# Two layers on one core: layer 0 split into a front and a back, with the dense steps of two batches dealt out over the stages

## The chip, the core and the metric

The kernel runs on one core of a Trainium2 chip. The core has TensorE (PE, matrix products into PSUM; its weight loads are listed apart as PEld), VectorE (DVE), ScalarE (ACT), GpSimd (POOL), SyncE (SP, which issues most DMAs here) and 16 DMA engines. Each engine works through its own list of instructions in order, and semaphores hold an instruction back until its inputs are there. PSUM has eight banks of 512 float32 columns. All data are float32, and each float32 product appears in the trace as two passes of PE.

The metric is the time of one execution on the device in microseconds; the median of three runs stands for a kernel.

## What is computed

The input x has 4 batches of 512 tokens with 256 features. Two layers follow one another:

```python
xn = _layernorm(x)
x = x + _L0_attn_ref(xn, ...) + _L0_ffn_ref(xn, ...)     # layer 0
xn = _layernorm(x)
x = x + _L1_attn_ref(xn, ...) + _L1_ffn_ref(xn, ...)     # layer 1
```

Layer 0's attention is linear: q, k and v are projections of xn; phi is elu + 1; the running sum of phi(k)·v over the tokens is multiplied by phi(q), scaled by 0.25 and projected by Wo. Layer 0's second part scores each token against 512 genes (logits = xn·Wc), keeps the 32 largest, takes their softmax, mixes the 32-wide gene vectors with it, and forms tanh(mix·Wd)·xn·(mix·Wu)·scale.

Layer 1's first part projects to q, k, v, forms running sums of exp(k)·v and exp(k), divides them, multiplies by sigmoid(q), and sends the result through a gated unit of width 1024. Its second part is a shared gated unit of width 352 and a choice of 2 among 16 experts of width 176 for each token.

## The kernel before, in words

Tokens stand on the 128 partitions, so that a batch has four tiles of 128 tokens. `xs` holds x and every result added to it; x of batch 0 is loaded first (`load_x(0)`, L110), then the weights, and x of batches 1 to 3 behind all weights (L148-149). SP's queue ends with a write of zeros to the 6016 KB of expert rows in DRAM (L173). Weights that layer 0 alone needs are in pool `wp`, on the right side of SBUF, and layer 0's working tiles in the pools `io0` (two buffers of each name) and `one0` (one).

The work is written as Python generators that yield after each step:

- `layer0(b, i0, nt)` (L224) does layer 0 for nt tiles of batch b from tile i0. It takes statistics (L194: bn_stats, bn_aggr, a square root on ACT) and normalises (L211), transposes by PE (`turn`, L217, its matmuls on L221) and copies to `xnT`. Then, tile by tile: `logits` (L286: two products of 512 columns, L289, copied by ACT to `lg`, of which there are two buffers); `top` (L296: four rounds of MAX8 and MATCH_REPLACE8 on DVE, L301 and L302, the exponential on ACT into a tile `e`, L307, and the masked sum, L309); a share of the attention parts `attend_kv` and `attend_q` (L265, L278: projections on L244, `phi` on ACT and DVE, a scan over the tokens on L271); and `express` (L313: four transposes of `e`, products with the genes, L321, and with Wd and Wu, L324, tanh, L326, a product on DVE, L329, and four elementwise operations on POOL, L331-334). `out` (L336) adds the projected context to `xs` for each tile at the end. Where a batch is cut in two, the running sum is handed on in `carry` (L275).
- `mix(b, i0, nt)` (L361) does layer 1 up to yT, the gate's input, and the choice of experts: statistics, normalise, transposes, q, k, v and the expert scores (L384), squares, exponentials (L410-411), four scans over transposed data (L421), reciprocals (L430) and the pick of two experts (L450-456).
- `dense(b, half, busy)` (L566) does the gated units of half a batch: 11 chunks (3 shared ones that read only the transposed xn of mix, then 8 that read yT). A chunk is an `up` (four products, L578, tanh on ACT, L582, a product on DVE, L584, and with `busy` a copy on ACT, L586, and a product on POOL, L587, else a product on DVE, L589) and, two chunks later, a `down` (L595). Its PSUM tiles `gu` are in `ps_d` (three banks) and `acc` in `ps_a` (one). Layer 0 and mix share the other four banks (`bank`, L188).
- `route`, `scatter`, `experts` and `combine` do the experts. Scatter's 32 DMAs and the loading of the expert weights are `paced`: each waits for the `down` that was written last before it.

`together` (L43) merges streams: it always takes the next step of the stream that has done the smallest share of the number given with it. The stages (L633-669) are:

```python
together(a(0, 0, 2))                              # a is layer0, m is mix, d is dense
together(m(0, 0, 2), a(0, 2, 2))
together(m(0, 2, 2), a(1, 0, 4), d(0, 0))
together(m(1, 0, 4), a(2, 0, 4), d(0, 1))
together(m(2, 0, 4), a(3, 0, 4), d(1, 0))
together(m(3, 0, 4), d(1, 1), (load_experts(), 17))
```

Between the second and third ACT halves two weight matrices (L636-639), and after the fifth the right side of SBUF is given to the expert weights (`first.close()`, L643, and a memset on POOL, L650). Then come routing with dense (2, ·), scatter with the rest of it, the experts, and combine with dense (3, ·).

What is written first has precedence, but the order on an engine is not exactly the order of the text: the framework that builds the program plans each engine's list ahead of time, and takes later work early where its inputs and its buffers should be there. The trace shows it: statistics of batch 1 (third stage) stand on DVE at 38.7 us, before batch 0 has been through mix.

Of the kernel before, what the change touches and what calls it, by code (L numbers as in the profile page):

```python
# [11 lines left out]
F32 = mybir.dt.float32  # L12
# [4 lines left out]
P = 128  # L17
# [36 lines left out]
def tile_two_layers(  # L54
# [47 lines left out]
    def load_x(b):  # L102
        nc.sync.dma_start(xs[:, b], x[b].rearrange("(t p) d -> p t d", p=P))
# [28 lines left out]
    nc.sync.dma_start(bob, bo0.partition_broadcast(P))  # L132
    wot = wp.tile([P, NH, D], F32, name="wot")
    nc.sync.dma_start(wot, wo0.rearrange("(h p) e -> p h e", p=P))

    w1 = const.tile([P, NH, 3 * D + NE], F32, name="w1")
    nc.sync.dma_start(w1[:, :, 0 : 3 * D], wqkv1.rearrange("(h p) e -> p h e", p=P))
# [48 lines left out]
    one = first.enter_context(tc.tile_pool(name="one0", bufs=1, side="right"))  # L186

    def bank():  # L188
        return ps_m.tile([P, L], F32, name="pm")
# [21 lines left out]
    def normalise(to, b, i0, nt, mv, rs):  # L211
        for i in range(nt):
            V.tensor_scalar(  # L213
                to[:, i], xs[:, b, i0 + i], mv[:, i, 0:1], rs[:, 0, i : i + 1], ALU.subtract, ALU.mult
            )

    def turn(src, nt, at):  # L217

        pt = bank()
        for i in range(nt):  # L220
            T.transpose(pt[:, i * P : (i + 1) * P], src[:, i, at : at + P], ident)  # L221
        return pt[:, 0 : nt * P]

    def layer0(b, i0, nt):  # L224

        W = nt * P
        mv, rs = statistics(io, b, i0, nt)
        xn = io.tile([P, NT, D], F32, name="xn")
        normalise(xn, b, i0, nt, mv, rs)

        sl = io.tile([P, 2, NT], F32, name="sl")
        V.tensor_scalar(sl[:, 0, 0:nt], rs[:, 1, 0:nt], rtemp, None, ALU.mult)
        V.tensor_scalar(sl[:, 1, 0:nt], rs[:, 1, 0:nt], scl, None, ALU.mult)
        yield
        xnT = io.tile([P, NH, L], F32, name="xnT")
        for h in range(NH):
            S.copy(xnT[:, h, 0:W], turn(xn, nt, h * P))
        yield


        def project(c):
            pm = bank()[:, 0:W]
            for h in range(NH):
                T.matmul(  # L244
                    pm,
                    wqkv[:, h, c * P : (c + 1) * P],
                    xnT[:, h, 0:W],
                    start=(h == 0),
                    stop=(h == NH - 1),
                )  # L250
            return pm

        def phi(c):

            pm = project(c)
            e = io.tile([P, L], F32, name="phi", bufs=3)[:, 0:W]
# [5 lines left out]
        ctxT = one.tile([P, NH, L], F32, name="ctxT")  # L262
        cums = {}

        def attend_kv(h):  # L265
            fk = phi(2 + h)
            pv = project(4 + h)
            kv = one.tile([P, L], F32, name="kv")[:, 0:W]
            V.scalar_tensor_tensor(kv, pv, bqkv[:, 4 + h : 5 + h], fk, ALU.add, ALU.mult)
            cum = io.tile([P, L], F32, name="cum")[:, 0:W]  # L270
            V.tensor_tensor_scan(  # L271
                cum, ones[:, 0:W], kv, carry[:, h : h + 1] if i0 else 0.0, ALU.mult, ALU.add
            )
            if i0 + nt < NT:
                V.tensor_copy(carry[:, h : h + 1], cum[:, W - 1 : W])  # L275
            cums[h] = cum

        def attend_q(h):  # L278
            fq = phi(h)
            V.scalar_tensor_tensor(ctxT[:, h, 0:W], fq, QSCALE, cums[h], ALU.mult, ALU.mult)  # L280


        rden = io.tile([P, NT], F32, name="rden")
        exT = one.tile([P, L], F32, name="exT")

        def logits(i):  # L286
            pl = bank()
            for h in range(NH):
                T.matmul(  # L289
                    pl, xnT[:, h, i * P : (i + 1) * P], wct[:, h], start=(h == 0), stop=(h == NH - 1)  # L290
                )
            lg = io.tile([P, NG], F32, name="lg")
            S.copy(lg, pl)  # L293
            return lg

        def top(i, lg):  # L296
# [12 lines left out]
            V.scalar_tensor_tensor(e, rep, TAKEN, e, ALU.is_equal, ALU.mult, accum_out=den)  # L309
            V.reciprocal(rden[:, i : i + 1], den)  # L310
            return e

        def express(i, e):  # L313
# [8 lines left out]
            S.copy(exT[:, i * P : (i + 1) * P], px[:, 0:P])  # L322
            du = bank()
            T.matmul(du, exT[:, i * P : (i + 1) * P], wdut, start=True, stop=True)  # L324
# [8 lines left out]
            G.tensor_tensor(xs[:, b, i0 + i], xs[:, b, i0 + i], bob, ALU.add)  # L333
            G.tensor_tensor(xs[:, b, i0 + i], xs[:, b, i0 + i], dn, ALU.add)

        def out(i):  # L336
            ao = bank()[:, 0:D]
            for h in range(NH):
                T.matmul(
                    ao, ctxT[:, h, i * P : (i + 1) * P], wot[:, h], start=(h == 0), stop=(h == NH - 1)  # L340
                )
            V.tensor_tensor(xs[:, b, i0 + i], ao, xs[:, b, i0 + i], ALU.add)


        parts = [lambda h=h, f=f: f(h) for h in range(NH) for f in (attend_kv, attend_q)]
        lg = logits(0)
        for i in range(nt):
            nxt = logits(i + 1) if i + 1 < nt else None
            e = top(i, lg)
            yield  # L350
            for part in parts[i * len(parts) // nt : (i + 1) * len(parts) // nt]:
                part()
            yield
            express(i, e)
            lg = nxt
            yield
        for i in range(nt):
            out(i)
            yield

# [260 lines left out]

    H = NC + 1

    def a(b, i0, nt):
        return layer0(b, i0, nt), 2 + 4 * nt

    def m(b, i0, nt):
        return mix(b, i0, nt), 6 + nt

    def d(b, half, busy=True):  # L630
        return dense(b, half, busy), H
# [12 lines left out]

    we = ctx.enter_context(tc.tile_pool(name="we", bufs=1, side="right"))
# [226 lines left out]
```

## Time and profile before

The three timed runs gave 593.17, 593.67 and 596.4 us. The profiled execution is another one:

| | us |
|---|---|
| median of the timed runs | 593.67 |
| the profiled execution's own time | 600.39 |
| its span, from first to last instruction | 598.7 |
| PE busy in the span | 541.2 |
| DVE busy in the span | 375.1 |
| first instruction of PE (L221) | 9.2 |
| first `top` of tile 0 / of tile 2 of batch 0 | 14.5 / 53.4 |
| last operation of mix of batch 3 (L432) ends | 344.1 |
| last dense (2, ·) product, end of the scatter's stage | 400 |
| experts begin / combine begins | 410 / 528 |

Busy time is time in which an engine has an instruction under way; matmuls overlap, and their ends are modelled, so that a busy PE is not always at its pace. Idle time has a releaser: what ended the wait. The chain of waits goes back from the last instruction, at each step to what released it; in it PE has 60% of the span, DVE 23%, ACT 6%, DMA 4% and POOL 2%. The largest groups are the dense products (L578, 125.6 us busy), those of the experts (L735, 64.8 us) and the downs (L595, 66.5 us). On DVE, MAX8 and MATCH_REPLACE8 of `top` take 685 and 675 ns each, 64 times each.

### The profile page before, as it was taken

What the parts mean: (1) busy time and instruction counts of PE and PEld (TensorE: products, weight loads), DVE (VectorE), ACT (ScalarE), POOL (GpSimd) and SP (SyncE); (2) the same over time, 40 slices, a digit from 0 to 9 for tenths busy, and PEclk for the clock granted to TensorE, in tenths of its full rate; (3) what the DMA queues carried; (4) which work ended last, traced back from release to release, by engine and by line L of the source; (5) the groups of instructions that cost most, each with busy time, mean ns of one, the idle gap of its engine ahead of it and who ended that gap; (6) DMA issues with size and microseconds to landing.
All of it is one profiled execution on the core that took longest, in us unless ns stands there. A gap on an engine that the chain in (4) does not pass through costs nothing.

```text
span 598.7 us, 7339 instructions
## 1 busy us (share of the span) xinstructions
PE 541.2 (90%) x2384; PEld 394.7 (66%) x2384; DVE 375.1 (63%) x992; ACT 233.1 (39%) x528; POOL 171.8 (29%) x214
## 2 busy tenths in 40 slices
PE   3557899989999999999999999898999999997796
PEld 1334665658566775667767788675777777785585
DVE  4979999997896888968923982231222222234552
ACT  2454755743556525565247111113333333321010
POOL 1234223252221532214532126650000000036640
PEclk9688999999999999999999999997999999999899
DMA  5993000000000000000086502223333332124431
GB/s 160 384 380 112 1 1 1 2 0 1 1 1 0 1 1 1 1 1 1 1 246 184 150 10 96 89 88 109 115 106 108 108 106 80 53 80 123 125 105 36
DMA packets 38373, 47.39 MB, mean 79 GB/s; under 512 B 3936, under 2 KB 34880, under 8 KB 38080
## 3 DMA queue, kind: packets, MB, share of 16 engines
q1 hardware_dynamic: 35264, 38.53, 19.9%
q0 software_dynamic: 3072, 8.39, 4.5%
q8 instruction: 20, 0.33, 0.2%
q14 instruction: 17, 0.14, 0.1%
HBM read 28.30 MB, written 18.61 MB: 78 GB/s over the span
## 4 chain that ended last, share of the span: by engine, by line
PE 60%; DVE 23%; ACT 6%; issue 4%; DMA 4%; POOL 2%; SPq 0%; DVEq 0%; ACTq 0%; POOLq 0%
PE gu L578 16%; PE pu L735 10%; PE acc L595 9%; PE py L756 7%; PE pm L384 5%; PE pt L698 4%; PE pm L244 3%; DVE sums L430 3%; DVE rep L302 3%; DVE top L301 3%; PE pm L289 2%; DVE sums L421 2%; DMA xg<-yrows,slot 2%; PE pm L324 2%; DVE xn L213 1%
## 5 line engine op out<-in xcount | busy, mean ns | idle before, releaser
L578 PE MATMUL gu<-yT,wugt 128*128 128x256 f32 x512 | 125.6, 381 | 0.0
L578 PEld LDWEIGHTS gu<-yT,wugt 128*128 128x128 f32 x512 | 95.2, 190 | 19.5 <-issue 7.4
L582 ACT ACTIVATE th<-gu 128x256 f32<-128x256 f32 (+1 forms) x88 | 32.9, 382 | 131.1 <-PE gu L578 85.5
L595 PE MATMUL acc<-wot,hid 128*128 128x256 f32 x256 | 66.5, 386 | 10.4 <-issue 4.5
L802 POOL DMA_INDIRECT xg<-yrows,slot x32 | 30.3, 948 | 144.9 <-DVE hid L589 130.8
L584 DVE SCALAR_TENSOR_TENSOR th<-th,gu 128x256 f32<-128x256 f32 (+1 forms) x88 | 35.9, 411 | 56.1 <-ACT th L582 50.8
L735 PE MATMUL pu<-wex,xgT 128*128 x188 | 64.8, 467 | 0.0
L595 PEld LDWEIGHTS acc<-wot,hid 128*128 128x128 f32 x256 | 47.7, 190 | 22.5 <-issue 6.7
L587 POOL TENSOR_TENSOR hid<-hid,th 128x256 f32<-128x256 f32 (+1 forms) x44 | 33.7, 770 | 95.6 <-ACT hid L586 95.6
L244 PE MATMUL pm<-xnT,wqkv 128*128 128x512 f32 (+1 forms) x120 | 46.7, 529 | 4.7 <-ACT lg L293 1.7
L744 DVE TENSOR_TENSOR hb<-pu,hb 128x176 f32<-128x176 f32 x47 | 16.1, 341 | 50.7 <-ACT hb L743 50.7
L578 PE MATMUL gu<-xn1T,sgu 128*128 128x256 f32 (+1 forms) x192 | 47.8, 393 | 0.0
L384 PE MATMUL pm<-w,xn1T 128*128 128x512 f32 (+1 forms) x128 | 45.8, 501 | 0.0
L756 PE MATMUL py<-wex,hgT 128*128 x188 | 44.5, 379 | 0.0
L756 PEld LDWEIGHTS py<-wex,hgT 128*128 128x128 f32 x188 | 35.6, 190 | 8.6 <-issue 0.2
L578 PEld LDWEIGHTS gu<-xn1T,sgu 128*128 128x128 f32 (+1 forms) x192 | 35.6, 189 | 7.3 <-issue 0.9
L735 PEld LDWEIGHTS pu<-wex,xgT 128*128 128x128 f32 x188 | 32.7, 194 | 10.2 <-issue 0.5
L384 PEld LDWEIGHTS pm<-w,xn1T 128*128 128x128 f32 x128 | 24.6, 193 | 22.2 <-issue 19.0
L244 PEld LDWEIGHTS pm<-xnT,wqkv 128*128 128x128 f32 x120 | 23.8, 201 | 22.6 <-issue 13.7
L748 DVE COPY hgT<-pt 128x512 f32<-128x512 f32 (+1 forms) x24 | 16.3, 680 | 34.9 <-PE pt L698 34.9
L544 POOL DMA_INDIRECT xrows<-xn,slot x32 | 30.9, 967 | 25.1 <-DVE cpair L538 9.7
L301 DVE MAX8 top<-rep 128x8 f32<-128x512 f32 x48 | 32.8, 685 | 0.4
(162 smaller groups left out, 881.2 us busy)
## 6 DMA issues: line engine op xcount, KB each, us to landing
xrows<-zero SPq DMA_DIRECT2D x1, 6016.0 KB, 22.6
xg<-xrows SPq DMA_DIRECT2D x23, 256.0 KB, 2.7
yrows<-yg SPq DMA_DIRECT2D x23, 256.0 KB, 2.1
wex<-in_w_gate_up_dram SPq DMA_DIRECT2D x8, 704.0 KB, 4.5
xs<-in_x_dram SPq DMA_DIRECT2D x4, 512.0 KB, 7.9
wugt<-in_wug_dram SPq DMA_DIRECT2D x1, 2048.0 KB, 12.2
wex<-in_w_down_dram SPq DMA_DIRECT2D x4, 512.0 KB, 4.9
out_dram<-xs SPq DMA_DIRECT2D x4, 512.0 KB, 2.9
```

Of the source, the lines that this page charges most:

```text
L244: T.matmul(pm, wqkv[:, h, c * P : (c + 1) * P], xnT[:, h, 0:W], start=(h == 0), stop=(h == NH - 1),)
L301: V.max(tp[:, 8 * r : 8 * r + 8], src)
L384: T.matmul(o[:, 0:n], xnT[:, h, i * P : (i + 1) * P], w1[:, h, at : at + n], start=(h == 0), stop=(h == NH - 1),)
L544: sc = G.indirect_dma_start(out=xrows, out_offset=bass.IndirectOffsetOnAxis(ap=slot[:, k, i : i + 1], axis=0), in_=xn1[:, i // NT, i % NT] ...
L578: T.matmul(gu[0:m, k], w[:, h, at : at + m], ins[which][:, h], start=(h == 0), stop=(h == NH - 1))
L582: S.activation(th[0:m], gu[0:m, 0], AF.Tanh, scale=0.5)
L584: V.scalar_tensor_tensor(th[0:m], th[0:m], 1.0, gu[0:m, 0], ALU.add, ALU.mult)
L587: G.tensor_tensor(hid[0:m], hid[0:m], th[0:m], ALU.mult)
L595: mm = T.matmul(acc[:, t], hid[0:m, t * P : (t + 1) * P], dw[0:m, dc], start=(n == 0 and t == 0), stop=(n == NC - 1), skip_group_check=True,)
L735: T.matmul(pg[:, 0 : 2 * NI], xT[:, i, h], wex[:, bass.ds(at[i] + h * 2 * NI, 2 * NI)], start=(h == 0), stop=(h == NH - 1),)
L756: mm = T.matmul(py[:, i * D : (i + 1) * D], hT[:, i, h], wex[:, bass.ds(at[i] + EW - (2 - h) * D, D)], start=(h == 0), stop=(h == 1),)
L802: G.indirect_dma_start(out=y, out_offset=None, in_=yrows, in_offset=bass.IndirectOffsetOnAxis(ap=slot[:, k, n : n + 1], axis=0),).ins
```

## The change

Layer 0 becomes two generators. `front(b, wide)` does statistics, normalise, transposes, the four logits and the whole attention up to `ctxT` for a full batch of 512 tokens, and yields ten times; it leaves xn, the slopes `sl`, `ctxT` and the four `lg` in a dictionary. `back(b, i0, nt)` takes them up and does top, express and out for nt tiles, in 3·nt steps, with the top of a tile ahead of the express of the tile before. So batch 0 is no longer cut in two for its front, only for its back and for mix.

The buffers change with it: `lg` has six, and the exponential is written over `lg` in place of `e`; `ctxT` has two, `cum` one, `kv` goes over the buffer of phi. With `wide`, which the first two fronts have, the projections go to the banks of `ps_d` instead of the four shared ones.

x of batch 1 is loaded ahead of the weights of layer 1. The stages are dealt anew; the dense work of batches 0 and 1 is one chain of 48 steps, of which the stages take 6, 8, 10, 15 and 9:

```diff
     wot = wp.tile([P, NH, D], F32, name="wot")
     nc.sync.dma_start(wot, wo0.rearrange("(h p) e -> p h e", p=P))
+    load_x(1)
...
-    for b in range(1, B):
+    for b in range(2, B):
         load_x(b)
...
+        def project(c):
+            if wide:
+                pm = ps_d.tile([P, 2, HB], F32, name="gu").rearrange("p i c -> p (i c)")
+            else:
+                pm = bank()
...
-            lg = io.tile([P, NG], F32, name="lg")
+            lg = io.tile([P, NG], F32, name="lg", bufs=6)
             S.copy(lg, pl)
-            return lg
+            lgs.append(lg)
...
+        for h in range(NH):
+            for i in (2 * h, 2 * h + 1):
+                logits(i)
+                yield
+            attend_kv(h)
+            yield
+            attend_q(h)
+            yield
+
+    def back(b, i0, nt):
+        xn, sl, ctxT, lgs = halfway[b]
...
-                    e = io.tile([P, NG], F32, name="e")
-                    S.activation(e, lg, AF.Exp, bias=nm, scale=sl[:, 0, i : i + 1])
+                    S.activation(lg, lg, AF.Exp, bias=nm, scale=sl[:, 0, i : i + 1])
...
-        for i in range(nt):
-            nxt = logits(i + 1) if i + 1 < nt else None
-            e = top(i, lg)
-            yield
-            for part in parts[i * len(parts) // nt : (i + 1) * len(parts) // nt]:
-                part()
-            yield
-            express(i, e)
-            lg = nxt
-            yield
-        for i in range(nt):
+        top(i0)
+        yield
+        for i in range(i0, i0 + nt):
+            if i + 1 < i0 + nt:
+                top(i + 1)
+                yield
+            express(i)
+            yield
+        for i in range(i0, i0 + nt):
             out(i)
             yield
...
-    together(a(0, 0, 2))
-    together(m(0, 0, 2), a(0, 2, 2))
+    def f(b, wide=False):
+        return front(b, wide), 10
+
+    def k(b, i0=0, nt=NT):
+        return back(b, i0, nt), 3 * nt
+
+    f0, f1 = front(0, True), front(1, True)
+    run_all(islice(f0, 4))
+    k0 = back(0, 0, 2)
+    together((f0, 6), (islice(k0, 2), 2))
+    together((k0, 4), (islice(f1, 4), 4))
+    together(m(0, 0, 2), (f1, 6))
...
-    together(m(0, 2, 2), a(1, 0, 4), d(0, 0))
-    together(m(1, 0, 4), a(2, 0, 4), d(0, 1))
-    together(m(2, 0, 4), a(3, 0, 4), d(1, 0))
+    dd = chain(dense(0, 0, True), dense(0, 1, True), dense(1, 0, True), dense(1, 1, True))
+
+    def some(n):
+        return islice(dd, n), n
+
+    together((chain(back(0, 2, 2), mix(0, 2, 2)), 14), some(6))
+    together(k(1), f(2), some(8))
+    together(m(1, 0, 4), k(2), f(3), some(10))
+    together(m(2, 0, 4), k(3), some(15))
     first.close()
...
-    together(m(3, 0, 4), d(1, 1), (load_experts(), 17))
+    together(m(3, 0, 4), (dd, 9), (load_experts(), 17))
```

More of the change, by code (lines that the diff above doesn't have):

```diff
@@ L185, in tile_two_layers @@
     io = first.enter_context(tc.tile_pool(name="io0", bufs=2, side="right"))
-    one = first.enter_context(tc.tile_pool(name="one0", bufs=1, side="right"))
     def bank():
@@ L222, in turn, with front @@
         return pt[:, 0 : nt * P]
-    def layer0(b, i0, nt):
-        W = nt * P
-        mv, rs = statistics(io, b, i0, nt)
+    halfway = {}
+    def front(b, wide):
+        mv, rs = statistics(io, b, 0, NT)
         xn = io.tile([P, NT, D], F32, name="xn")
-        normalise(xn, b, i0, nt, mv, rs)
+        normalise(xn, b, 0, NT, mv, rs)
         sl = io.tile([P, 2, NT], F32, name="sl")
-        V.tensor_scalar(sl[:, 0, 0:nt], rs[:, 1, 0:nt], rtemp, None, ALU.mult)
-        V.tensor_scalar(sl[:, 1, 0:nt], rs[:, 1, 0:nt], scl, None, ALU.mult)
+        V.tensor_scalar(sl[:, 0], rs[:, 1], rtemp, None, ALU.mult)
+        V.tensor_scalar(sl[:, 1], rs[:, 1], scl, None, ALU.mult)
         yield
@@ L236, in layer0 @@
         for h in range(NH):
-            S.copy(xnT[:, h, 0:W], turn(xn, nt, h * P))
+            S.copy(xnT[:, h], turn(xn, NT, h * P))
         yield
+        ctxT = io.tile([P, NH, L], F32, name="ctxT")
+        lgs = []
+        halfway[b] = (xn, sl, ctxT, lgs)
         def project(c):
-            pm = bank()[:, 0:W]
+            if wide:
+                pm = ps_d.tile([P, 2, HB], F32, name="gu").rearrange("p i c -> p (i c)")
+            else:
+                pm = bank()
             for h in range(NH):
[L244 to L250, printed above, removed]
+                T.matmul(pm, wqkv[:, h, c * P : (c + 1) * P], xnT[:, h], start=(h == 0), stop=(h == NH - 1))
             return pm
@@ L255, in phi @@
             pm = project(c)
-            e = io.tile([P, L], F32, name="phi", bufs=3)[:, 0:W]
+            e = io.tile([P, L], F32, name="phi", bufs=3)
             S.activation(e, pm, AF.Relu, bias=nbqk[:, c : c + 1], scale=-1.0)
@@ L260, in phi @@
             return e
-        ctxT = one.tile([P, NH, L], F32, name="ctxT")
         cums = {}
         def attend_kv(h):
-            fk = phi(2 + h)
+            kv = phi(2 + h)
             pv = project(4 + h)
[L268 to L276, printed above, removed]
+            V.scalar_tensor_tensor(kv, pv, bqkv[:, 4 + h : 5 + h], kv, ALU.add, ALU.mult)
+            cums[h] = io.tile([P, L], F32, name="cum", bufs=1)
+            V.tensor_tensor_scan(cums[h], ones, kv, 0.0, ALU.mult, ALU.add)
         def attend_q(h):
             fq = phi(h)
-            V.scalar_tensor_tensor(ctxT[:, h, 0:W], fq, QSCALE, cums[h], ALU.mult, ALU.mult)
-        rden = io.tile([P, NT], F32, name="rden")
-        exT = one.tile([P, L], F32, name="exT")
+            V.scalar_tensor_tensor(ctxT[:, h], fq, QSCALE, cums[h], ALU.mult, ALU.mult)
         def logits(i):
@@ L291, in logits, with top @@
                 )
-            lg = io.tile([P, NG], F32, name="lg")
+            lg = io.tile([P, NG], F32, name="lg", bufs=6)
             S.copy(lg, pl)
-            return lg
-        def top(i, lg):
+            lgs.append(lg)
[9 more added lines that the diff above has]
+        xn, sl, ctxT, lgs = halfway[b]
+        rden = io.tile([P, NT], F32, name="rden")
+        def top(i):
+            lg = lgs[i]
             tp = io.tile([P, NACT], F32, name="top")
@@ L305, in top, with express @@
                     V.tensor_scalar(nm, tp[:, 0:1], sl[:, 0, i : i + 1], -1.0, ALU.mult, ALU.mult)
-                    e = io.tile([P, NG], F32, name="e")
-                    S.activation(e, lg, AF.Exp, bias=nm, scale=sl[:, 0, i : i + 1])
+                    S.activation(lg, lg, AF.Exp, bias=nm, scale=sl[:, 0, i : i + 1])
             den = io.tile([P, 1], F32, name="den")
-            V.scalar_tensor_tensor(e, rep, TAKEN, e, ALU.is_equal, ALU.mult, accum_out=den)
+            V.scalar_tensor_tensor(lg, rep, TAKEN, lg, ALU.is_equal, ALU.mult, accum_out=den)
             V.reciprocal(rden[:, i : i + 1], den)
-            return e
-        def express(i, e):
+        def express(i):
+            e = lgs[i]
             pw = bank()
@@ L321, in express @@
                 T.matmul(px[c * GD : (c + 1) * GD, 0:P], gn[:, c], wT[:, c], start=True, stop=True)
-            S.copy(exT[:, i * P : (i + 1) * P], px[:, 0:P])
+            exT = io.tile([P, P], F32, name="exT")
+            S.copy(exT, px[:, 0:P])
             du = bank()
-            T.matmul(du, exT[:, i * P : (i + 1) * P], wdut, start=True, stop=True)
+            T.matmul(du, exT, wdut, start=True, stop=True)
             dn = io.tile([P, D], F32, name="dn")
@@ L332, in express @@
             G.tensor_tensor(dn, dn, xw, ALU.mult)
-            G.tensor_tensor(xs[:, b, i0 + i], xs[:, b, i0 + i], bob, ALU.add)
-            G.tensor_tensor(xs[:, b, i0 + i], xs[:, b, i0 + i], dn, ALU.add)
+            G.tensor_tensor(xs[:, b, i], xs[:, b, i], bob, ALU.add)
+            G.tensor_tensor(xs[:, b, i], xs[:, b, i], dn, ALU.add)
         def out(i):
@@ L341, in out @@
                 )
-            V.tensor_tensor(xs[:, b, i0 + i], ao, xs[:, b, i0 + i], ALU.add)
-        parts = [lambda h=h, f=f: f(h) for h in range(NH) for f in (attend_kv, attend_q)]
-        lg = logits(0)
-        for i in range(nt):
-            nxt = logits(i + 1) if i + 1 < nt else None
-            e = top(i, lg)
-            yield
-            for part in parts[i * len(parts) // nt : (i + 1) * len(parts) // nt]:
-                part()
-            yield
-            express(i, e)
-            lg = nxt
-            yield
-        for i in range(nt):
+            V.tensor_tensor(xs[:, b, i], ao, xs[:, b, i], ALU.add)
+        top(i0)
[5 more added lines that the diff above has]
+            express(i)
+            yield
+        for i in range(i0, i0 + nt):
             out(i)
@@ L622, in tile_two_layers @@
     H = NC + 1
-    def a(b, i0, nt):
-        return layer0(b, i0, nt), 2 + 4 * nt
     def m(b, i0, nt):
         return mix(b, i0, nt), 6 + nt
-    def d(b, half, busy=True):
-        return dense(b, half, busy), H
-    together(a(0, 0, 2))
-    together(m(0, 0, 2), a(0, 2, 2))
+    def f(b, wide=False):
[8 more added lines that the diff above has]
+    together(m(0, 0, 2), (f1, 6))
     for c in range(0, DFF // P, 2):
```

## The prediction

> **What bounds the kernel now.** I read the totals and the forty slices first, then a table of windows cut at the stages, then TensorE's timeline, and last the chain of waits.
>
> ```profile
> PE 541.2 (90%) x2384; PEld 394.7 (66%) x2384; DVE 375.1 (63%) x992; ACT 233.1 (39%) x528; POOL 171.8 (29%) x214
> ...
> PE   3557899989999999999999999898999999997796
> ...
> DVE  4979999997896888968923982231222222234552
> ...
> PEclk9688999999999999999999999997999999999899
> ```
>
> PE is the busiest engine, and its low digits stand in the first four slices (15 us each), where VectorE (DVE) is high. The third row is the granted clock, low in the same place. The table of windows (columns: length, then busy us and instructions of PE, weight loads, DVE, ACT, POOL, then the clock):
>
> ```profile
> 10.35:23.41 13.06, 7.84 (x20) 4.38 (x21) 9.34 (x28) 5.68 (x10) 4.20 (x6) 0.88 0.73 269
> 23.41:37.65 14.24, 11.74 (x52) 7.68 (x52) 10.82 (x29) 7.30 (x17) 3.19 (x5) 0.75 1.08 376
> 37.65:60.00 22.35, 13.15 (x34) 7.26 (x34) 21.47 (x74) 8.90 (x21) 8.61 (x11) 0.80 0.56 200
> 60.00:146.00 86.00, 80.64 (x360) 53.08 (x359) 82.07 (x230) 45.65 (x101) 29.33 (x40) 0.99 0.00 1
> 146.00:222.00 76.00, 73.32 (x323) 49.27 (x322) 63.60 (x157) 40.05 (x90) 23.21 (x29) 1.00 0.00 1
> ...
> 297.00:345.00 48.00, 46.08 (x206) 35.32 (x205) 27.23 (x69) 23.62 (x60) 14.18 (x21) 1.00 0.61 181
> ```
>
> A busy PE need not be at its peak, so I counted. Two lines of the chain give the pace of back-to-back passes (a float32 product is two passes):
>
> ```profile
> 167.96 1.72 PE pm L289 x4
> ...
> 347.37 1.73 PE gu L578 x8
> ```
>
> That is 0.43 us for 512 columns (L289) and 0.216 us for 256 (L578); likewise 0.23 for 272, 0.16 for a transpose, 0.11 for L321. Passes of each shape times these give PE's **least time** in a window: 146 to 222 us holds 76.9 us of work, 222 to 297 holds 76.5, 60 to 146 holds 84.0, 297 to 345 holds 46.3. So from 60 us until layer 0 and mix of all batches are done (345 us), PE is full. Before 60 us it does only 27.2 us of work, and 1.2 us more are missing up to 83. So the head of the kernel loses about **34 us** of PE time, and an idle PE there is paid in full at the end, because what follows is a full PE.
>
> The timeline of PE shows the largest hole (in brackets the idle time before, and what ended it):
>
> ```profile
> 37.05 0.60 PE L221 MATMUL pm<-ident,xn 128*128 128x128 f32 x4
> 43.46 1.23 PE L221 MATMUL pm<-ident,xn 128*128 128x128 f32 x4 [5.80 <-DVE xn L213]
> 44.48 5.17 PE L289 MATMUL pm<-wct,xnT 128*128 128x512 f32 x8
> ```
>
> and that of ACT what followed it:
>
> ```profile
> 49.39 0.21 ACT L207 ACTIVATE rs<-rs 128x8 f32<-128x8 f32 x1 [4.30 <-DVE rs L206]
> 49.51 0.57 ACT L293 COPY lg<-pm 128x512 f32<-128x512 f32 x1
> ```
>
> At 37 us the second half of batch 0 has its transposes, but its logits (L289) stand behind the transposes of mix(0,0,2), which wait 5.80 us for DVE's normalise. Then its logits' copies stand on ACT behind a square root for a later batch. Its first top-8 starts at 53.37 us. The second half was normalised at 10.06 us: for 40 us its work was there and was not reached. An earlier hole (5.23 us before L316 at 23.41) waits for the first top 32.
>
> **What the change removes, adds and moves.** PE's and DVE's sums over the whole kernel hardly move. For batch 0 alone, pairs of 256-column operations become one of 512 (phi 2 x 0.47 to 0.73, scan 2 x 0.69 to 1.21, kv and ctxT likewise), and two carry copies of 0.15 and one set of small statistics go: some 3 us of DVE. Nothing is added to PE. From passes times pace, and for DVE from start to start in its timeline (MAX8 0.60, MATCH_REPLACE8 0.66 with its value load, reciprocal 1.66), the pieces are:
>
> front, one batch: PE 8 transposes 1.3 + 16 logit passes 6.9 + 24 projection passes 10.4 = 18.6; DVE 13 (5 for statistics, normalise and slopes, 8 for phi, kv, scan, context).
> back, one batch: PE 16 transposes 2.5 + 32 passes L321 3.5 + 8 of L324 3.5 + 16 of L339 3.5 = 13; DVE 4 tops of 6.4 + 3.9 = 29.5.
> mix: PE 15.7, DVE 24.5. Dense half: PE 11 steps of 12 passes of 0.216 = 28.5; DVE 4.7.
>
> Four batches and four halves give PE 303 and DVE 287 (the windows show 283 busy). The old order needs, before its first dense half is due, a(0,0,2), a(0,2,2) and m(0,0,2): DVE 54, PE 39. The new order has front 0, half of back 0, front 1 and m(0,0,2) there: DVE 53, PE 51. **For the same DVE time PE gets 12 us more work early**, because a front gives 18.6 us of PE for 13 of DVE, a back 13 for 29.5.
>
> The new head, step by step. Batch 0 is normalised by 10.3 us (10.14 now). Eight transposes and two copies of 512 (0.59 each) put the first logits at 12.3: lost 12.3. The first eight passes took 5.25 us instead of 3.46 (clock): lost 1.8. The other logits and projections, 13.9 us, then run to about 31. On DVE the two tops and the attention parts (12.8 + 7.9) run from 15.6 to 36.3, and the statistics and normalise of batch 1 (5) to 41.5. Express of two tiles gives PE some 4 us in that time, so of 31 to 41.5 I count 6 lost. From 42 PE has front 1 (18.6), mix(0,0,2) (7.8) and the shared chunks of dense (0,0), which need only the transposes of mix (3 x 2.6): more than the 21 us to 63. For friction there I take 2. Sum 12.3 + 1.8 + 6 + 2 = 22 instead of 34: **gain 12 us**. The hole of 31 to 41.5 has two ends: none of it, if batch 1's statistics slip in early (they did in the old run, at 38.7, before older work), or all 10; friction lies between 0 and the 7 us that DVE sat idle from 10 to 38 us in the old head (13.06 - 9.34 and 14.24 - 10.82). So the gain lies between 20 and 3; I take 12, nearest to the row-by-row sum.
>
> Edits with no price: batch 1's 512 KB ahead of layer 1's weights delays these by some 1.4 us (at 380 GB/s); w1 is first read at 49 us, and DMA has ended by 53, so cover remains; without it 1.4 us. The order of SP's queue is otherwise the same, and POOL's instructions are the same ones. Exponentials in place of e: one buffer less, the same instructions. Projections of the first two fronts in the dense banks: these banks are idle until 60 us. The dense steps dealt as 6, 8, 10, 15, 9 instead of 12 a stage: PE/DVE by stage is then 28/30, 50/46, 71/71, 66/60 and 37/28 us, against 76/72 in the old full stages, which ran in 76 and 75 us.
>
> Two rules of the Trainium skill bear on this. The row first: passes at full pace fill 101% of 146 to 222 us. The Trainium skill ("Perfetto Trace Analysis", Identifying the Most-Contended Engine) says that matmul busy time misleads and weight-load busy time is the measure; that is 66% here and would leave PE a third of slack, with DVE the bound and a gain near 0. The count of passes decides against it: a weight load of 0.19 us under a pass of 0.43 us cannot fill the time. The second: the clock is 0.75 to 0.88 in 10 to 60 us, around holes of 5.2 and 5.8 us. The Trainium skill ("TensorE: Matmul & The Clock Gate", What's actually happening) says an idle window of about 3.4 us halves the clock until a busy one; if the hole of 31 to 41.5 stays, that would take some 1.7 us off my gain.
>
> **Rivals.**
> Tail given back. Mix of batch 3 keeps 9 dense steps instead of 12. Its chain took 48 us (297 to 345) with PE full; 37 us of PE work would leave it half uncovered by three steps, 7.8 us, unless dense (2,0) is drawn forward. For it: dense (2,0) starts only at the very end now. Against it: it does start at 338 us, ahead of routing. Time: 593.7 - 12 + 7.8 = 589.5.
> The hole only moves. The head is DVE's, whose work is the same; if tops keep ahead of batch 1's statistics and mix waits behind front 1, the gain is 0 to 3: 592.
> Slower. Six lg buffers serve four logits of the batch in back and four of the next front. So the third and fourth logits of a front wait for an express of the batch before; their copy stands on ACT, which is in order, ahead of the exponentials that the next top's end needs. One such wait costs up to a top, 6.4 us; there are two in each of three batches, 38 us at worst. It decides the sign from two full ones on; half of all is 19: 593.7 - 12 + 19 = 601. For it: ACT did wait 4.3 us in order at 49 us. Against it: buffers are handed out in planned order, and the copies of logits wait for PE alone now (15.3 us over 12 waits).
>
> **The numbers.** The profiled execution took 600.39 us, span 598.7 and 1.7 around it; the median of the three timed runs is 593.67, so 6.7 less. I take the difference in span over to the median: 593.7 - 12 = 581.7. Chances: forecast (574 to 588) 0.62, tail 0.14, hole moves 0.12, slower 0.12. The range reaches from a gain of 20 with 3 for luck in the tail (571) to just past no change (596), leaving out the slow case and a little below. A measurement here can tell 0.5%, 3 us, from no change: faster 0.75 (forecast and most of tail), same 0.14, slower 0.11.
>
> **What would show it.** PE's slices 2 to 4 rise to 7 or more, the clock with them; PE does some 40 to 45 us of least work by 60 us instead of 27; tops of tiles 2 and 3 follow early; no 5 us wait of L221 at 37 to 43. From 65 us to the end of mix(3) PE stays full, and that end comes at about 333 instead of 344 us; all behind it keeps its length. I am wrong if the least work by 60 us is below 32, if ACT's lg copies wait for DVE, or if PE shows holes in the last mix.

## The result and the profile after

| | before | after |
|---|---|---|
| median of six runs, taken beside one another, us | 594.15 | 599.16 |
| ratio after to before, 95% interval | | 1.0079 [1.0058, 1.0099] |
| span of the profiled execution, us | 598.7 | 597.9 |
| PE busy, DVE busy, us | 541.2, 375.1 | 543.4, 365.3 |

The change makes the kernel 5.0 us slower, where I had forecast 12 us less; the time lies 3 us above my range (571 to 596). Kernels ran some 8 us longer in two of the four groups of runs below (before took 602 us instead of 594), and the profiled execution of before (600.39 us) is a longer one too, with the extra time behind the first scatter, so each kernel is compared with the runs of before of its own group, and of a profile marked * below only what lies ahead of that point.

The totals and slices of the profile after (15 us a slice):

```profile
PE 543.4 (91%) x2360; PEld 391.8 (66%) x2360; DVE 365.3 (61%) x973; ACT 236.9 (40%) x521; POOL 171.0 (29%) x214
...
PE   3959969999989999999989969997999999997796
...
DVE  3999997999967789924943785331222222235552
...
PEclk9968979999989999999999979997999999999999
```

Slices 2 to 4 of PE are 9, 5, 9 instead of 5, 5, 7: better, though the third is not the 7 that I had named. And there are new low digits, the sixth (75 to 90 us) and the twenty-fourth (345 to 360 us), and the clock is low there too. The windows (columns as in the prediction) give these places:

```profile
10.35:23.41 13.06, 12.20 (x28) 5.81 (x29) 8.35 (x23) 7.20 (x11) 4.18 (x6) 1.00 0.84 273
...
60.00:75.00 15.00, 14.69 (x43) 7.43 (x42) 15.00 (x59) 11.28 (x25) 2.26 (x2) 1.00 0.00 1
75.00:90.00 15.00, 10.42 (x52) 6.41 (x52) 14.27 (x31) 6.08 (x14) 4.34 (x6) 0.77 0.00 0
...
345.00:360.00 15.00, 11.44 (x44) 9.74 (x45) 12.96 (x32) 1.15 (x3) 2.28 (x7) 0.77 0.00 0
```

In the first window PE was busy 7.84 us before. For the other two holes, the same windows of before:

```profile
345.00:360.00 15.00, 15.00 (x71) 13.15 (x71) 12.77 (x39) 2.31 (x6) 3.70 (x6) 1.00 0.06 19
60.00:75.00 15.00, 13.49 (x65) 9.19 (x64) 14.69 (x46) 10.72 (x26) 3.99 (x5) 0.96 0.00 1
75.00:90.00 15.00, 14.01 (x66) 9.13 (x64) 15.00 (x49) 8.07 (x15) 4.42 (x7) 1.00 0.01 1
```

The least time of the work that PE has behind it is, in us, passes of each shape in the trace times the pace of that shape, as in the prediction. Here each pass is counted once, where it starts; windows that are added up count a pass across a cut twice, so that before has 26.1 us of work at 60 us and not 27.2. Two profiles of one kernel differ by up to 1.6 us in this count at 300 us.

| until | 60 | 75 | 90 | 105 | 300 | 345 | 360 |
|---|---|---|---|---|---|---|---|
| before | 26.1 | 39.5 | 53.8 | 69.1 | 263.8 | 307.6 | 322.5 |
| after | 36.1 | 50.4 | 59.5 | 72.7 | 266.4 | 307.8 | 317.3 |
| lead of after | 10.0 | 10.9 | 5.7 | 3.6 | 2.6 | 0.2 | -5.2 |

So the head brings 11 us by 75 us, close to the 12 worked out. Half of it is gone by 90 us, some 3 us reach the last mix, and from there to 360 us after loses 8 us more. What stands in the last hole shows in PE's timeline of after:

```profile
339.70 1.35 PE L580 MATMUL gu<-xn1T,sgu 128*128 128x256 f32 x5
341.19 1.13 PE L597 MATMUL acc<-wot,hid 128*128 128x256 f32 x4
342.15 1.46 PE L580 MATMUL gu<-xn1T,sgu 128*96 128x256 f32 x6
348.56 1.19 PE L597 MATMUL acc<-sdn,hid 128*128 128x256 f32 x2 [4.95 <-DVE hid L591]
```

and DVE's of the same time:

```profile
340.44 2.33 DVE L423 TENSOR_TENSOR_SCAN sums<-ones,pm 128x512 f32<-128x512 f32 x2
...
343.86 3.35 DVE L432 RECIPROCAL sums<-sums 128x256 f32<-128x256 f32 x2
347.13 0.36 DVE L586 SCALAR_TENSOR_TENSOR th<-th,gu 128x256 f32<-128x256 f32 x1
347.40 0.68 DVE L434 TENSOR_TENSOR yT<-sums 128x512 f32<-128x512 f32 x1
348.00 0.42 DVE L591 TENSOR_TENSOR hid<-gu,th 128x256 f32<-128x256 f32 x1
```

The nine dense steps of this stage are used up, three chunks of dense (2, 0) are drawn forward, and then PE has nothing: the products of these chunks (L586, L591) stand on DVE behind the scans and reciprocals of the last mix. (L580, L597, L586, L591 are the lines 578, 595, 584, 589 of before.)

From here to the experts the main points are, in us: the starts of the last add of layer 0, of the last yT, of the first and the last scatter DMA, and of the weight load of the first expert product.

| kernel | last add of layer 0 | last yT of mix | scatter | first expert product |
|---|---|---|---|---|
| before * | 294.4 | 343.5 | 356.3 to 401.7 | 409.3 |
| after | 299.3 | 347.4 | 361.3 to 403.3 | 410.8 |
| 12 and 12 | 292.2 | 339.6 | 352.4 to 394.2 | 401.7 |
| 12 and 12 (second time) | 293.5 | 340.8 | 353.7 to 395.5 | 402.4 |
| late tops | 296.5 | 344.6 | 358.5 to 400.6 | 408.2 |
| before with 15 and 9 | 299.3 | 348.3 | 362.2 to 404.3 | 412.0 |
| 9 and 15 * | 289.1 | 338.6 | 353.5 to 400.8 | 408.4 |
| 12 and 12, late tops (second time) | 291.2 | 338.5 | 351.4 to 393.2 | 400.8 |
| after, 24 scatters | 298.2 | 346.3 | 360.2 to 401.0 | 408.6 |
| after, 4 chunks fewer * | 298.7 | 346.8 | 360.7 to 404.0 | 411.6 |
| after, both fewer * | 298.8 | 346.9 | 361.0 to 395.5 | 403.2 |

### The profile page after: what moved, and what is told of

Same layout as the page of the kernel before. It is cut to its first block, busy times and chain, and to the rows that moved or that the text cites. A ratio compares the mean times of both kernels' runs of the same rounds, so it can differ in the third digit from the quotient of the medians.

```text
span 597.9 us, 7249 instructions
## 1 busy us (share of the span) xinstructions
PE 543.4 (91%) x2360; PEld 391.8 (66%) x2360; DVE 365.3 (61%) x973; ACT 236.9 (40%) x521; POOL 171.0 (29%) x214
## 4 chain that ended last, share of the span: by engine, by line
PE 56%; DVE 27%; DMA 5%; POOL 4%; ACT 4%; issue 3%; SPq 0%; POOLq 0%; DVEq 0%; ACTq 0%
PE gu L580 14%; PE pu L747 10%; PE acc L597 7%; PE py L768 7%; PE pm L386 5%; DVE rep L309 5%; DVE top L308 4%; PE pt L710 4%; DMA xg<-yrows,slot 3%; DVE sums L432 3%; PE pm L221 2%; PE pm L331 2%; DVE sums L423 2%; PE pm L280 2%; PE pm L252 1%
## 5 line engine op out<-in xcount | busy, mean ns | idle before, releaser
L580 PE MATMUL gu<-yT,wugt 128*128 128x256 f32 x512 | 125.3, 381 | 0.8 <-ACT hid L588 0.8
L580 PEld LDWEIGHTS gu<-yT,wugt 128*128 128x128 f32 x512 | 95.8, 191 | 16.3 <-issue 3.1
L597 PE MATMUL acc<-wot,hid 128*128 128x256 f32 x256 | 66.6, 384 | 8.1 <-DVE hid L591 7.0
L586 DVE SCALAR_TENSOR_TENSOR th<-th,gu 128x256 f32<-128x256 f32 (+1 forms) x88 | 36.0, 410 | 57.8 <-ACT th L584 57.8
L589 POOL TENSOR_TENSOR hid<-hid,th 128x256 f32<-128x256 f32 (+1 forms) x44 | 32.8, 746 | 118.5 <-ACT hid L588 118.5
L597 PEld LDWEIGHTS acc<-wot,hid 128*128 128x128 f32 x256 | 47.1, 190 | 19.3 <-DVE hid L591 9.0
L580 PE MATMUL gu<-xn1T,sgu 128*128 128x256 f32 (+1 forms) x192 | 47.7, 393 | 0.0
L386 PE MATMUL pm<-w,xn1T 128*128 128x512 f32 (+1 forms) x128 | 44.6, 494 | 0.0
L580 PEld LDWEIGHTS gu<-xn1T,sgu 128*128 128x128 f32 (+1 forms) x192 | 35.5, 189 | 7.1 <-issue 0.7
L747 PEld LDWEIGHTS pu<-wex,xgT 128*128 128x128 f32 x188 | 32.7, 194 | 10.2 <-issue 0.5
L221 PE MATMUL pm<-ident,xn 128*128 128x128 f32 x64 | 14.0, 357 | 20.6 <-DVE xn L213 20.5
L309 DVE MATCH_REPLACE8 rep<-top,rep 128x512 f32<-128x512 f32 x48 | 32.3, 674 | 0.0
```

Source lines behind the costliest of these rows:

```text
L386: T.matmul(o[:, 0:n], xnT[:, h, i * P : (i + 1) * P], w1[:, h, at : at + n], start=(h == 0), stop=(h == NH - 1),)
L580: T.matmul(gu[0:m, k], w[:, h, at : at + m], ins[which][:, h], start=(h == 0), stop=(h == NH - 1))
L586: V.scalar_tensor_tensor(th[0:m], th[0:m], 1.0, gu[0:m, 0], ALU.add, ALU.mult)
L589: G.tensor_tensor(hid[0:m], hid[0:m], th[0:m], ALU.mult)
L597: mm = T.matmul(acc[:, t], hid[0:m, t * P : (t + 1) * P], dw[0:m, dc], start=(n == 0 and t == 0), stop=(n == NC - 1), skip_group_check=True,)
L747: T.matmul(pg[:, 0 : 2 * NI], xT[:, i, h], wex[:, bass.ds(at[i] + h * 2 * NI, 2 * NI)], start=(h == 0), stop=(h == NH - 1),)
```

## The experiments

Three theories. **A**: the last mix starts late because 39 instead of 36 dense steps stand ahead of it, and from its start to the experts a chain of fixed length follows (from the last add of layer 0 to the last yT some 48 us, routing 13, scatter 42). **B**: PE is the bound throughout, and what counts is only how long it is idle, so that closing the hole at 343 us gives the time back. **C**: the lead of the head is lost because DVE takes the tops of tiles 2 and 3 ahead of the first mix. Every kernel was timed in five rounds beside before.

**1. After, 12 and 12.** The dealing of the last two stages as it was in before:

```diff
-    together(m(2, 0, 4), k(3), some(15))
+    together(m(2, 0, 4), k(3), some(12))
...
-    together(m(3, 0, 4), (dd, 9), (load_experts(), 17))
+    together(m(3, 0, 4), (dd, 12), (load_experts(), 17))
```

> The changed kernel with the dense steps dealt as 6, 8, 10, 12, 12 instead of 6, 8, 10, 15, 9, so that the last mix has 12 beside it as before the change; all else as changed. Theory A (chain): from the end of batch 3's layer 0 the time to the experts is a fixed chain (mix 48 us, routing 13 us, scatter 40 us), and three dense steps (7.8 us of PE) put ahead of it push its start, from 294.7 to 300.0 us. Then this start comes back to about 293 to 295 us, and the time falls by 4 to 7 us, to 592 to 595. Theory B (PE): PE is full up to the experts, so it does not matter on which side of that start a dense step stands; 599 within 1.5 us, or slower.

Measured: 590.32 us beside 593.56, ratio 0.9949 [0.9932, 0.9967]. Run once more in a later group, it gave 590.49 beside 594.05:

> The kernel after with 12 and 12 dense steps in the last two stages, run once more beside the kernel with both edits, so that the two are compared with the same runs of before: a ratio of about 0.995 as at first.

Ratio 0.9942 [0.9921, 0.9962]. The last add of layer 0 comes 7.1 and 5.8 us earlier than in after (the two profiles), for three steps of 2.59 us, and everything to the experts moves with it (first expert product 9.1 and 8.5 us earlier). This one edit turns 0.8% slower into 0.5% faster, better than A had expected.

**2. After, dense (2, 0) with its product on POOL.** For the first half of batch 2, the copy on ACT and the product on POOL take the place of DVE's product L591:

```diff
-    d2 = chain(dense(2, 0, False), dense(2, 1, False))
+    d2 = chain(dense(2, 0, True), dense(2, 1, False))
```

> The changed kernel with the first half of batch 2's dense work in the busy form (copy on ACT and product on POOL instead of a product on DVE). Theory B (PE, with the tail as its hole): the hole of 4.95 us of PE at 343.6 us, where the downs of dense (2,0) wait for a product that stands on DVE behind the last mix's reciprocals, goes, and the time falls by 4 to 5 us. Theory A (chain): the hole lies beside the chain; routing still waits for the last yT, and the 32 scatters of 1.27 us each still take 40 us from there; 599 within 1.5 us.

Measured: 602.17 us, 1.0131 [1.0105, 1.0156]. The hole did not close: PE now waits 4.34 us for ACT's copy, since L586 stays on DVE behind the reciprocals. And POOL, which now has products among the scatter DMAs, takes 44.8 us for these instead of 42.0, from a first scatter that is 1.1 us later: about the 3 us by which this kernel is slower than after. So this says nothing on B, only that POOL's time beside the scatter is dear.

**3. After, late tops.** The first MAX8 of the tops of tiles 2 and 3 is ordered on DVE behind the normalise of the first mix; nothing else changes:

```diff
...
-                V.max(tp[:, 8 * r : 8 * r + 8], src)
+                mx = V.max(tp[:, 8 * r : 8 * r + 8], src)
+                if r == 0 and b == 0 and i >= 2:
+                    tc.add_manual_dep(mx.ins, held[(0, 0)], ...)
...
-        normalise(xn, b, i0, nt, mv, rs)
+        held[(b, i0)] = normalise(xn, b, i0, nt, mv, rs).ins.name
```

> The changed kernel with the tops of tiles 2 and 3 of batch 0 ordered on DVE behind the normalise of mix(0,0,2) (an order only, no semaphore). In the changed kernel these tops (12.8 us) run at 38 to 57 us, ahead of mix(0,0,2), whose normalise comes at 60.7 us. Theory C (the lead of 11 us at 75 us is lost because DVE was given to these tops): the normalise moves to about 50 us, the dense steps start at about 65 instead of 74 us, PE's least work by 105 us rises from 75 to 80 us or more, and the time falls by 4 to 6 us. Theory A alone without C: DVE is full there either way, so only the order changes; within 1.5 us of 599.

Measured: 595.19 us, 1.0028 [1.0015, 1.0041], some 3 us less than after (0.5% by the ratios). The normalise of the first mix comes at 52.70 instead of 60.67 us, and the lead at 90 us is 10.2 instead of 5.7. But the first dense product does not come earlier (75.1 against 74.0 us), by 105 us PE has 75.3 us of work behind it, less than the 80 that I had expected, and at 300 us the lead is 5.0 instead of 2.6. C explains most of the lead lost by 90 us, some 2.5 us of the lead at 300 us and 3 us of the time, not the whole loss.

**4. Before, 15 and 9.** The price of the dealing alone, without the new head: three dense steps of before are moved from the last stage to the one ahead of it.

```diff
-    together(m(2, 0, 4), a(3, 0, 4), d(1, 0))
+    d11 = dense(1, 1, True)
+    together(m(2, 0, 4), a(3, 0, 4), (chain(dense(1, 0, True), islice(d11, 3)), 15))
...
-    together(m(3, 0, 4), d(1, 1), (load_experts(), 17))
+    together(m(3, 0, 4), (d11, 9), (load_experts(), 17))
```

> The kernel before the change, with one thing of it: the first three steps of the dense half that stands beside the last mix are moved into the stage before (15 and 9 instead of 12 and 12). Theory A: batch 3's layer 0 ends later by up to 7.8 us and the chain behind it is fixed, so the time rises by 4 to 6 us, to 598 to 600, as slow as the changed kernel. Theory B: PE does the same work in another order, 594 within 1.5 us.

Measured: 601.8 us, 1.0138 [1.0112, 1.0165], 8.2 us more than before. With experiment 1 the sum closes: the dealing costs 8.2 us by itself, the rest of the change gives 3.2, together the 5.0 of the result (each to within 1 or 2 us). The last add comes 4.9 us and the first scatter 5.9 us later than in before, and PE's hole in the last mix is there, as in after and not with 12 and 12:

```profile
349.49 1.19 PE L595 MATMUL acc<-sdn,hid 128*128 128x256 f32 x2 [4.95 <-DVE hid L589]
```

**5. Both edits, 6. and 7. other dealings of the tail, 8. an earlier dealing.** The four ran in one group, where before took 601.99 us. The fifth joins the edits of 1 and 3:

> The kernel after with 12 and 12 dense steps in the last two stages and with the tops of tiles 2 and 3 of batch 0 behind the normalise of the first mix. Theory A (the chain from the last out add to the scatter has a fixed length, so what is ahead of it counts) and theory C (the early tops cost 4 us of lead) together: the gains of both runs add, 8.8 and 4.0 off 599.2, so 586 to 587; last out add at about 288.5. If the tail now hides the lead (PE bound behind 290), it stays at 589 to 590.

Ratio 0.9904 [0.9867, 0.994]. Run again beside the second run of 1:

> The kernel with both edits (12 and 12 dense steps, late tops), run once more beside the one with 12 and 12 alone. Theory C: its first scatter was 2.4 us earlier, so 2 to 3 us less than that kernel, a ratio to before of 0.990 to 0.991. If the late tops are worth nothing with this dealing: 0.995.

587.63 us, ratio 0.9883 [0.9851, 0.9915]: 2.9 us less than with 12 and 12 alone, first scatter 2.3 us earlier. This version beats both kernels, by 6.4 us and 11.5 us. Most of the gain of the late tops remains, and the last mix has no hole. PE's timeline of this kernel, where after has its wait of 4.95 us (its L606, L589 and L598 are the lines 597, 580 and 589 of after; L497 is the first product of routing):

```profile
332.30 1.13 PE L606 MATMUL acc<-wot,hid 128*128 128x256 f32 x4 [0.28 <-POOL hid L598]
333.27 1.89 PE L589 MATMUL gu<-xn1T,sgu 128*128 128x256 f32 x8
336.05 1.13 PE L606 MATMUL acc<-wot,hid 128*128 128x256 f32 x4 [0.89 <-POOL hid L598]
337.01 3.19 PE L589 MATMUL gu<-xn1T,sgu 128*128 128x256 f32 x14
340.04 0.66 PE L497 MATMUL pr<-chosen,stri 128*128 128x256 f32 x2
```

The sixth takes after and deals 9 and 15 in the last two stages:

> The kernel after with 9 and 15 dense steps in the last two stages in place of 15 and 9. A chain of one length whatever runs beside it: three steps fewer than with 12 ahead of it, 7.8 us off 590.3, so 582 to 583. Theory A with its bound: beside the chain there is room for some 104 us of PE work and no more, three steps make it full, so what the earlier start gives the longer mix takes back: 588 to 592. Theory B (PE alone, order of no matter): 590 as well, but with the last out add at 284 to 285 and the last yT no earlier than 337.

Ratio 0.9997 [0.9969, 1.0025], some 3 us behind 12 and 12. A chain of one length whatever runs beside it falls: the mix takes 49.5 us instead of 47.4. The last add comes only 3.1 to 4.4 us earlier for three steps fewer. By the prediction's own sums DVE could be why: mix(2) and the last back have 28.7 us of PE and 54 of DVE, twelve steps (28.5 us) make it 57 and 59, nine some 50 and 58. But the trace does not bear this out for the whole stage: in this run DVE is full from 222 to 240 us and then busy 35.2 of the 49 us to 289, where PE is busy 47.3. What holds the last add back stays open. The seventh has both edits with 10 and 14:

> As the kernel with both edits, but 10 and 14 dense steps in the last two stages in place of 12 and 12. If the chain still has slack of PE beside it, 2 x 2.6 us less than that kernel (581 to 582); if PE is full there, the same to 1 us more.

Ratio 0.9908 [0.9873, 0.9943], the same as both edits with 12 and 12: the room is used up. The eighth has both edits and deals 9, 9, 6 in the first three stages with dense steps, in place of 6, 8, 10:

> As the kernel with both edits, but the first three stages with dense steps take 9, 9 and 6 in place of 6, 8 and 10 (the same 24). If the rest of the lead is lost between 75 and 120 us because PE has no dense steps at hand while DVE does the tops, PE does 2 to 4 us more least work by 120 us, the last out add comes 2 to 4 us earlier, and so does the end. If DVE's own work sets the pace there, the lead is the same (5 us at 300) and the time within 1 us of the kernel with both edits, or above it for DVE's part of the extra steps.

Ratio 0.9908 [0.9875, 0.9941], the same again. PE is 2.0 us further by 120 us and 1.1 us further by 300 than in the first profile of both edits, the latter within what two profiles of one kernel differ by. A lack of dense steps at hand is not where the rest of the lead goes.

**9. to 12. What holds the end behind the last mix.** The last 8 of the 32 scatter DMAs are left out, in after and in before:

```diff
-            for i in range(NTT):
+            for i in range(NTT if k == 0 else NTT // 2):
...
-    together((scatter(), 33), (d2, 2 * H - 6))
+    together((scatter(), 25), (d2, 2 * H - 6))
```

> The kernel after with the last 8 of the 32 scatter DMAs left out (the second choice of tokens 1024 to 2047 is not sent to its expert; the experts find zeros there). Theory A (in after the tail is the chain, with about 8 us of PE slack beside it): 8 x 1.27 = 10.1 us off the chain, PE becomes the bound after some 8, so 7 to 9 us less than after, 590 to 592, a ratio to before of 0.994 to 0.997. Theory B (PE bound in the tail): 0 to 2 us less than after, 597 to 599.

597.72 us, 1.0063 [1.004, 1.0086], only 1 us less than after, which is within the noise. The scatter as the sole bound falls: PE, full from 349.5 us on with the rest of dense (2, ·), ends at the same time as the scatter. But the two are not independent, as the scatter is paced by the `down`s: in after 9 of its 32 DMAs wait for one (5.3 us in all), and with 8 left out 14 of the 24 do (15.8 us). So the 24 take 40.8 us from the first start to the last, where the 32 took 42.0, and the edit hardly shortened the path.

> The kernel before with the same 8 scatter DMAs left out. Theory A with its balance (in before the chain of 104 us and 104 us of PE work beside it end together): the DMAs are not alone the bound, so 0 to 3 us less than before, a ratio of 0.995 to 1.0. If in before, too, the chain alone set the end: 10 us less, a ratio of 0.983.

591.79 us, 0.996 [0.9936, 0.9984], as A had it for before; but there, too, 14 of the 24 DMAs wait for a `down` (15.6 us), and with the run above this no longer tells the kernels apart. So I left out four chunks of dense (2, 1), 10.4 us of PE, first alone and then with the 8 DMAs:

```diff
...
+        mine = chunks[0 : NC - 4] if (b, half) == (2, 1) else chunks
         hids = []
-        for n, c in enumerate(chunks):
+        for n, c in enumerate(mine):
...
-    together((scatter(), 33), (d2, 2 * H - 6))
+    together((scatter(), 33), (d2, 2 * H - 10))
```

> The kernel after with the last 4 of the 11 chunks of dense (2, 1) left out (4 x 2.59 = 10.4 us of PE; batch 2's second half lacks these parts of its gated unit). Two paths of equal length behind the last mix, routing with scatter (55 us) and the rest of dense (2, .) (22 steps, 57 us): taking from one alone gives 0 to 3 us, so 596 to 599. PE alone as the bound: 8 to 10 us less, 589 to 591.

Ratio 1.003 [1.0007, 1.0054] (603.92 us beside 601.78), against 1.0079 for after.

> The kernel after with both left out, the 4 chunks of dense (2, 1) and the last 8 scatter DMAs (the second choice of tokens 1024 to 2047 is not sent). Two paths of equal length: only now the end comes earlier, by 8 to 10 us, 589 to 591, a ratio of 0.991 to 0.995 to before. Something third behind both (the expert weights' load, the experts' first gather): 595 or more.

Ratio 0.9852 [0.9817, 0.9887] (593.63 us). Taking 8 DMAs away gives 0.2%, four chunks 0.5%, both together 2.3%, some 13 us. That is more than I had expected and more than the 10.4 us taken from PE; up to the first expert product the profiles show 7.6 us (410.8 to 403.2), and where the rest comes from stays open, as after itself wasn't timed in that group. Two paths that end together run behind the last mix, tied to each other by the waits for the `down`, and neither alone is the bound. In PE's timeline of the kernel with four chunks fewer, PE is done with dense (2, 1) and stands before the first transposes of the experts until the scatter has landed:

```profile
396.19 2.75 PE L597 MATMUL acc<-wot,hid 128*128 128x256 f32 x12
398.77 2.32 PE L580 MATMUL gu<-xn1T,sgu 128*128 128x256 f32 x10
409.45 1.09 PE L711 MATMUL pt<-ident,xg 128*128 128x128 f32 x4 [8.36 <-DMA xg<-xrows]
```

With both fewer, dense (2, 1) ends at 393.1 us and those transposes begin at 401.0. What theory A keeps: both paths begin when the last mix ends, so that its end counts in full. What it loses: the scatter is not the bound by itself. B is right in that PE's lost time in the last mix is lost; but the hole was not closed in any run without also starting the mix earlier, so how much of the 8 us is the late start and how much the hole is not told apart. Routing ahead of the end of the mix (its choices stand at 327.4 us in after, and its first operation starts at 348.2, behind the last yT) wasn't tried.

## Why the prediction was wrong, point by point

**The step that failed** is the one that priced the edits at nothing: "The dense steps dealt as 6, 8, 10, 15, 9 instead of 12 a stage: PE/DVE by stage is then 28/30, 50/46, 71/71, 66/60 and 37/28 us, against 76/72 in the old full stages". I compared sums of PE and DVE for each stage, and in the last stage 37 and 28 us look cheap. But the last mix is a chain that took 47 to 49.5 us in every run of the table, as the rival had it. A stage of 37 us of work in 48 us of chain leaves 11 us of PE with no work of its own; chunks drawn forward fill a part, and 8 us of lead are lost between 300 and 360 us. The three steps also lengthen the stage ahead of it, which was full. Measured, this costs 8.2 us (before with 15 and 9), where the step had 0 and the rival 7.8. (The step's 66 us are also mis-added: 28.7 us and 15 steps at 28.5 us for 12 make 64.)

Of the 17.5 us between the forecast (581.7) and the result (599.2), 8.2 are this step, 8.8 are the gain of the head (12 in the sum, 3.2 at the end), and 0.5 is the base, whose median is now 594.15.

**The rival "tail given back"** had the place, the mechanism and the size, and I gave it 0.14. What spoke against it, that dense (2, 0) is drawn forward, is true for three chunks and no more: their products stand behind the mix on DVE. In before, too, three chunks are drawn forward, from 338 us. There the steps of the stage itself last until 341 us (the last product starts on POOL at 340.21) of a mix that ends at 344; in after they last as long (340.41), but the mix ends at 348. I had read a start, not how much could follow. The rival's time, 589.5, was wrong only for the second failure.

**The gain of the head** was mis-sized at the end, not at its own place. The sum gave 12 us by 63 to 75 us; the count shows 10.9. The first logits stand at 12.65 us (12.3 worked out), and PE is busy 12.20 of the 13.06 us behind 10.35. The hole that I had put at 31 to 41.5 us is there:

```profile
37.81 2.08 PE L331 MATMUL pm<-wdut,exT 128*128 128x512 f32 x2 [0.38 <-ACT exT L329]
44.21 0.71 PE L221 MATMUL pm<-ident,xn 128*128 128x128 f32 x2 [4.33 <-DVE xn L213]
```

The granted clock is 0.50 in the windows from 36 to 48 us, 12 us and not the single window of some 3.4 us from which the prediction's estimate, 1.7 us off the gain, came.

What failed is the sentence that "From 65 us to the end of mix(3) PE stays full", and with it "an idle PE there is paid in full at the end". Lead that is left at 300 us is worth about its size: 12 and 12 has 4.1 and 2.7 us of it in its two profiles and is 3.2 and 3.6 us faster than before. But some 8 of the 11 us never get there. DVE's timeline of after shows the first part of the loss:

```profile
37.67 0.66 DVE L308 MAX8 top<-lg 128x8 f32<-128x512 f32 x1
...
60.67 0.72 DVE L213 TENSOR_SCALAR xn<-xs,mv,rs 128x256 f32<-128x256 f32 x2
```

The planner takes the top of tile 2, written two stages later, as soon as its logits are there, ahead of the mix that PE will need at 75 us. I had sums for "DVE 53" with two tops in it; four ran. Holding these back returned some 3 us, with either dealing. In the versions with late tops, whose lead at 90 us is 10 us, 3 to 5 us more are lost before the last mix. It is not the dense dealing of the early stages (experiment 8). A part goes with the granted clock, which differs between profiles of one kernel. From 60 to 146 us it is 0.94 in the second profile of both edits, 0.98 in the first and 1.00 in experiment 8, and the lead at 300 us is 4.9, 6.5 and 7.6 us; 12 and 12 has 0.98 and 1.00 with 2.7 and 4.1 us, after 0.96 with 2.6. No run changes the clock alone, so its share is not shown. DVE is busy 79.0 to 80.6 of those 86 us with both edits, less than in before (82.07), and whether it holds the rest stays open.

**The slower rival** (third and fourth logits waiting for `lg` buffers) is not there: all 14 waits of ACT before the copy of the logits, 20.6 us, end with PE's logits and none with DVE. Slower came by another mechanism. "The hole only moves" gave 592. The head did gain 11 us at its own place, so it is wrong there, though near in the net gain; that tops get ahead of what PE needs did come true, for tiles 2 and 3 and the first mix.

**The edits at nothing that were so**: x of batch 1 ahead of the weights, and the projections in the dense banks, show no wait of their own on PE in the first 60 us: PE had 36.1 us of work done by then against 26.1. That is below the 40 to 45 that I had named, for the hole at 39.9 to 44.2 us and the clock of 0.75 in the window around it (37.65 to 60 us).

**The count of passes** held where PE had few waits: with each pass counted once, 146 to 222 us of before holds 76.4 us of work (76.9 in the prediction), so that weight loads, busy 66%, did not show the bound. The Trainium skill ("Perfetto Trace Analysis", Identifying the Most-Contended Engine) names a second measure beside weight-load busy time, the work done against the peak, which the prediction leaves out.

## What to carry to other kernels

A stage is as long as the longest of its engine sums and its chain; where filler work is dealt out over stages, write the chain's length beside the sums, above all for the last stage that can take filler, since too few steps there leave idle time that later work did not make up, and too many ahead of it delay it. Lead that is won early reaches the end only if every stage between can hold it: follow it by a count of work done, at several times, before calling it won. And where a planner reorders, work that becomes ready early may be run early, as the tops of tiles 2 and 3 were; if it is on a scarce engine, try holding it back by hand.

## What the runs showed of the hardware

An indirect DMA occupies POOL for 0.96 us and the next follows 0.30 us later (1.27 us from start to start), so that 32 of them make up most of a path of 42.0 us, as long as 16 dense steps of PE; the rest are waits for a `down`. With POOL's products among them it became 44.8.

The clock fell without a long wait. From 76 to 82 us of after, PE's longest waits are 1.57 and 1.28 us, with short matmuls between; the windows (columns as before) show the clock at half behind them:

```profile
76.00:79.00 3.00, 1.30 (x8) 0.94 (x9) 3.00 (x6) 2.62 (x7) 2.78 (x4) 1.00 0.00 0
79.00:82.00 3.00, 1.72 (x9) 1.19 (x7) 2.27 (x6) 0.00 (x0) 1.56 (x3) 0.59 0.00 0
82.00:85.00 3.00, 3.00 (x12) 2.35 (x10) 3.00 (x7) 0.46 (x1) 0.00 (x0) 0.50 0.00 0
85.00:88.00 3.00, 2.51 (x15) 1.00 (x14) 3.00 (x6) 1.22 (x5) 0.00 (x0) 0.77 0.00 0
```

The Trainium skill ("TensorE: Matmul & The Clock Gate", What's actually happening) has the half clock follow an idle window of some 3.4 us. Here PE was still busy 1.30 of the 3 us to 79 us, and the clock fell in the 3 us after them (0.59), with no idle stretch of that length before it.
